# Expert rows loaded by SyncE from a register address and turned by VectorE

## The chip, the cores and the metric

The kernel runs on one core of one Trainium2 chip. The metric is device time in microseconds (us) of one execution. Engines are called by their short names: PE (TensorE, matrix products; PEld is its weight load), DVE (VectorE), ACT (ScalarE), POOL (GpSimd) and SP (SyncE, which here only issues transfers and relays semaphores). Sixteen DMA engines move data between HBM, the chip's DRAM, and SBUF, the on-chip memory of 128 partitions. Transfers issued by SP go through a hardware queue (q1 in the profile), those issued by POOL through a software queue (q0). PSUM holds matrix results.

## The reference

Eight images of 256 channels x 32 x 32 pixels go through two layers. Layer 0 is attention with 8 heads over the pixels. Layer 1 is attention with one head, and then a mixture of experts: each of the 8 x 1024 tokens is sent to its two best experts out of eight.

```python
# layer 1, mixture of experts, on tokens of 256 values
logits = tokens @ router_w.T
rw, re = top_k(softmax(logits), 2)
rw = rw / maximum(rw.sum(-1), 1e-12)          # two gates per token
out = tokens
for e in range(8):
    h = gelu(tokens @ w1[e] + b1[e])          # 256 -> 256
    out = out + gate[:, e:e+1] * (h @ w2[e] + b2[e])   # 256 -> 256
```

All data are float32.

## The kernel before

The images are worked off one after the other (`for b in range(B)`): `layer0` is the attention with 8 heads, `attend` the attention with one head, `normed` and `dispatch` the normalisation and the routing. For the first seven images `dispatch` writes each token's row of 256 values to DRAM twice, with an indirect DMA by POOL, into `rows`, where each expert has a region of its own. The rows of the last scatter leave during `layer0` of image 7. Image 7 itself is worked densely at the end (`dense`: all eight experts).

Between `layer0` and `attend` of image 7 stands the stage that the change is about, `experts` (L1018). The rows of the seven images are cut into 63 blocks of 256 rows (`BR`, which is `R` = 2 times 128); a block belongs to one expert. `plan` (L926) has worked out on DVE, for every block, where its rows begin (`row_at`) and which expert's weights it needs (`w_at`). For each block:

- `fetch` (L1024) lets POOL gather the block's weights, 128 rows of 5128 bytes out of `wpack`, into one of four buffers (`wb_0` to `wb_2` and `wb_x`, chosen by `b % 4`). Where block b needs the same expert as block b-4, the indices are out of bounds and nothing is moved. Then POOL gathers the block's 256 rows into `xr` (three buffers), so that partition p holds rows 2p and 2p+1. Four PE transposes write them to PSUM (`px`, L1044), and DVE copies them to `xb` (L1046, two buffers): channels on the partitions, tokens along the row.
- `hidden` (L1049): four products give `ph` (L1054), ACT applies Gelu (L1064).
- `collect` (L1073): four products give `pe` (L1079), DVE adds the bias (`yb`, L1088), SP stores the block to `y` (L1093).

A float32 product of 128x128 by 128x256 shows as two MATMUL records in the profile, so `ph` and `pe` have 8 records per block each, and `px` has 4. The loop works one block ahead: at step b it traces `hidden(b-1)`, `fetch(b)`, `collect(b-2)`. PE's order through the stage is therefore ph(b-1), px(b), pe(b-2), ph(b), px(b+1), pe(b-1), and so on.

What sets the order: the program is traced in order, and a scheduler then gives each engine its own list, in which an instruction may move ahead of earlier ones that are not ready in the scheduler's model of time. On the chip each engine works its list strictly in order. `tc.issue_after(ins)` places what is traced in its block behind `ins` on the same engine, without a wait for its end.

Three other places matter. In `layer0` of images 1 to 7 SP relays a semaphore after each half group of products (`relay.nop()`, L551), and the next group's first product waits for it. `pack` (L281) fills `wpack` early in the program, on SP's queue behind 56 MB of zeros for `rows` (`fill`, L266): two transfers for w1 (L286), two for w2 (L291), one for b1, eight for b2 (L302). Behind these stand, on the same queue, the transfers of `attend` of image 0 (`aT`, L697), where a quarter of the squares that DVE transposed are moved between partitions by SP. DVE transposes 32x32 squares within each partition group (`nc.vector.transpose`, L690, L430, L1219).

Of the kernel before, what the change touches and what calls it, by code (L numbers as in the profile page):

```python
# [10 lines left out]
F32 = mybir.dt.float32  # L11
# [8 lines left out]
def kernel(  # L20
# [23 lines left out]
    nc = tc.nc  # L44
# [14 lines left out]
    WROW = NCC * FF + NFC * D + NFC + D  # L59
    NWB = 3  # L60
    NXB = NWB + 1

    dram = ctx.enter_context(tc.tile_pool(name="dram", bufs=1, space=bass.MemoryType.DRAM))
    const = ctx.enter_context(tc.tile_pool(name="const", bufs=1))
# [10 lines left out]
    def big(name):  # L75

        return ps_big.tile([P, 1024], F32, tag="big", name=name)
# [58 lines left out]
    for e in range(E):  # L136
# [15 lines left out]
    r_iota = const.tile([P, 1], F32, name="r_iota")  # L152
    nc.gpsimd.iota(
        r_iota, [[1, 1]], base=0, channel_multiplier=R, allow_small_or_imprecise_dtypes=True
    )
    ones = const.tile([P, P], F32, name="ones")
    nc.gpsimd.memset(ones, 1.0)

# [48 lines left out]


    NB = NT // NH2
    SQ = 32  # L210
    NQ = P // SQ

    def bcast(t, n):

# [66 lines left out]
    def pack():  # L281


        wp = wpack.rearrange("(e p) c -> e p c", p=P)
        for dc in range(NCC):
            nc.sync.dma_start(  # L286
                wp[:, :, ts(dc, FF)], w1.rearrange("e (dc p) f -> dc e p f", p=P)[dc]
            )
        at = NCC * FF
        for fc in range(NFC):  # L290
            nc.sync.dma_start(  # L291
                wp[:, :, at + fc * D : at + (fc + 1) * D],
                w2.rearrange("e (fc p) d -> fc e p d", p=P)[fc],
            )
# [142 lines left out]
    def layer0(b, xT, begun, routing, xs):  # L437
# [138 lines left out]
        for at in range(last + LAG + 1):  # L576
            g, j = steps[min(at, last)]

            early = at > LAG and j == 1 and (g, j) not in PROJECT
            if at <= last:  # L580
                with tc.issue_after(counted.ins) if counted else nullcontext():
                    score(at, 0, 0)
            if 0 < at <= last + 1:
                with tc.issue_after(counted.ins) if counted else nullcontext():
                    score(at - 1, 1, 1)
                second_max(at - 1, 1)
                soften(at - 1, 1)
            if at >= LAG:
                with tc.issue_after(counted.ins) if counted else nullcontext():
                    gather_values(at - LAG, 0)  # L590
                counted = None
            if at <= last:

                with tc.issue_after(seconds[1].ins) if 1 in seconds else nullcontext():
                    first_max(at, 0)
                score(at, 0, 1)
                score(at, 1, 0)
                second_max(at, 0)
                if not early:
                    soften(at, 0)  # L600
                with tc.issue_after(seconds[0].ins):
                    ahead = divide(at - 1) if at > 0 else seconds[0]
                with tc.issue_after(ahead.ins):
                    first_max(at, 1)
            elif at == last + 1:
                divide(last)
            if at == 0:
                begun.rest()
                share()
            if at >= LAG:  # L610
                array = gather_values(at - LAG, 1)
# [314 lines left out]
    def plan(group):  # L926
# [51 lines left out]
        nc.vector.tensor_copy(row_at[:, :nb], lo)  # L978
# [36 lines left out]
                ats.append(at)  # L1015
            group.kept[b] = gate, ats

    def experts(group):  # L1018
        n = group.n
        row_at, w_at = group.where  # L1020

        wbs_x = [*wbs, one.tile([P, WROW], F32, tag="v", name="wb_x")]

        def fetch(b):  # L1024
# [10 lines left out]
            nc.gpsimd.indirect_dma_start(  # L1035
                out=xr.rearrange("p r d -> p (r d)"),
                out_offset=None,
                in_=group.rows[:, :],
                in_offset=bass.IndirectOffsetOnAxis(ap=row_at[:, b : b + 1], axis=0),
            )  # L1040
            px = big(f"px_{n}_{b}")
            for dc in range(NCC):
                for r in range(R):
                    nc.tensor.transpose(px[:, ts(dc * R + r, P)], xr[:, r, ts(dc, P)], ident)  # L1044
            xb = two.tile([P, NCC, BR], F32, tag="xb", name=f"xb_{n}_{b}")
            nc.vector.tensor_copy(xb.rearrange("p c t -> p (c t)"), px[:, : NCC * BR])  # L1046
            return xb

        def hidden(b, xb):  # L1049
# [23 lines left out]
        def collect(b, hT):  # L1073
# [19 lines left out]
            nc.sync.dma_start(group.y[ts(b, BR), :].rearrange("(p r) d -> p r d", r=R), yb)  # L1093
            if b == NXB:
                with tc.issue_after(added.ins):
                    places(group)


        rows, hiddens = {}, {}
        for b in range(group.nb + 2):  # L1100
            if b - 1 in rows:
                hiddens[b - 1] = hidden(b - 1, rows.pop(b - 1))
            if b < group.nb:
                rows[b] = fetch(b)
            if b - 2 in hiddens:
                collect(b - 2, hiddens.pop(b - 2))

    class Results:

# [235 lines left out]
    for b in range(B):  # L1345
# [6 lines left out]
        if b + 1 < B:  # L1352
# [64 lines left out]
```

## Time and profile before

| what | us |
|---|---|
| median of 15 runs (lowest, highest) | 2361.88 (2359.56, 2366.89) |
| the profiled execution's own time | 2363.75 |
| its span from first to last instruction | 2361.6 |
| experts: first `ph` product to the last `pe` record (1877.5 to 2131.1) | 253.6 |
| from the first `ps` product of image 0's `attend` to that of image 1 | 248.0 |
| from the first `ps` product of image 1's `attend` to that of image 2 | 240.1 |

The profile's page gives busy time per engine and the chain of work that ended last; the trace can be asked for instructions in order of time, for the DMA queues in a stretch, and for busy shares in stretches. A busy PE record can overlap the next one, so the time that a group costs is read from the distance between starts, and not from the durations.

### The profile page before, as it was taken

The page shows a single profiled execution, that of the slowest core. Times are in us where ns is not written, and L with a number is a line of the kernel's source. Part 1 is how long each engine was busy: PE and PEld are TensorE (multiplying, and loading weights), DVE is VectorE, ACT ScalarE, POOL GpSimd, SP SyncE. Part 2 cuts the span into 40 slices and gives each one's busy share as a digit, 9 for nine tenths or more (in the row PEclk, how much of TensorE's full clock was granted, in tenths as well). Part 3 has the DMA queues.
Part 4 walks back from the last instruction along what each step waited for, and adds up shares of the span by engine and source line. Part 5 has one row for each costly group of instructions (what it writes and reads, how often), then busy time and mean ns, then how long its engine had stood idle before and what let it go on. Part 6 is the DMA issues. An engine that isn't in the chain of part 4 may idle for free.

```text
span 2361.6 us, 37255 instructions
## 1 busy us (share of the span) xinstructions
PE 2305.2 (98%) x13375; PEld 1256.6 (53%) x13375; DVE 1512.4 (64%) x3660; ACT 1092.4 (46%) x1954; POOL 421.3 (18%) x391
## 2 busy tenths in 40 slices
PE   9999999999999999999999999999999999999798
PEld 3345534653455345634563356335633588885465
DVE  5775577567855785578557855786578653334755
ACT  3663366346634663466346634663555422223311
POOL 0000012000200020002000200030003144444563
PEclk9999999999999999999999999999999999999899
DMA  8995201020102010201020102010201266655564
GB/s 295 385 386 140 63 17 39 13 50 15 41 10 54 12 44 7 57 10 46 4 60 6 50 1 50 17 35 1 45 19 63 86 223 215 206 195 145 154 176 110
DMA packets 219232, 209.23 MB, mean 89 GB/s; under 512 B 120200, under 2 KB 162856, under 8 KB 217256
## 3 DMA queue, kind: packets, MB, share of 16 engines
q1 hardware_dynamic: 192952, 139.13, 19.6%
q0 software_dynamic: 25008, 67.20, 9.2%
q8 instruction: 107, 1.75, 0.3%
q10 hardware_dynamic: 1088, 0.52, 0.1%
q14 instruction: 77, 0.63, 0.1%
HBM read 108.88 MB, written 110.90 MB: 93 GB/s over the span
## 4 chain that ended last, share of the span: by engine, by line
PE 89%; DVE 5%; DMA 2%; issue 2%; another core or an unknown queue 1%; ACT 1%; SPq 0%; DVEq 0%; ACTq 0%; POOLq 0%
PE po L541 19%; PE psc L464 19%; PE py L713 8%; PE ps L672 8%; PE pqk L346 7%; PE pr L638 5%; PE pv L383 4%; PE ph L1054 4%; PE pe L1079 4%; PE px L657 2%; PE pqk L324 2%; PE pdy L1307 2%; PE pdh L1283 2%; PE px L1044 1%
## 5 line engine op out<-in xcount | busy, mean ns | idle before, releaser
L505 ACT ACTIVATE ex<-psc,nmax 128x1024 f32<-128x1024 f32 x512 | 570.5, 1115 | 304.4 <-DVE scrap L488 218.0
L464 PE MATMUL psc<-qk,qk 64*64 64x512 f32 x4096 | 575.7, 593 | 7.8 <-ACT ex L505 7.7
L541 PE MATMUL po<-ex,vs 64*64 64x512 f32 x4096 | 569.7, 592 | 1.4 <-DVE vs L521 0.5
L488 DVE TENSOR_SCALAR_CACHE_REDUCE scrap<-psc,nmax 128x512 f32<-128x512 f32 x512 | 384.2, 750 | 161.2 <-PE psc L464 134.9
L479 DVE TENSOR_REDUCE nmax<-psc 128x1 f32<-128x512 f32 x512 | 350.3, 684 | 9.5 <-PE psc L464 9.5
L464 PEld LDWEIGHTS psc<-qk,qk 64*64 64x64 f32 x4096 | 179.3, 132 | 285.1 <-ACT ex L505 136.4
L541 PEld LDWEIGHTS po<-ex,vs 64*64 64x64 f32 x4096 | 174.3, 132 | 275.5 <-issue 85.0
L713 PE MATMUL py<-n,aT 128*128 128x256 f32 x1024 | 235.7, 384 | 7.5 <-DVE aT L706 3.9
L672 PE MATMUL ps<-nT,xa 128*128 128x512 f32 x512 | 228.6, 592 | 0.0
L713 PEld LDWEIGHTS py<-n,aT 128*128 128x128 f32 x1024 | 197.0, 193 | 59.2 <-issue 27.0
L917 POOL DMA_INDIRECT rows<-n,d_at x112 | 109.2, 975 | 660.8 <-DVE nmax L479 660.5
L844 POOL TENSOR_TENSOR t<-t,n 128x2048 f32<-128x2048 f32 x8 | 36.3, 4535 | 879.7 <-DVE n L238 879.7
L697 ACT COPY aT<-sq 32x256 f32<-32x256 f32 x384 | 154.4, 402 | 82.0 <-DVE sq L690 44.1
L346 PE MATMUL pqk<-xT,wqkv 128*128 128x512 f32 x384 | 171.2, 599 | 0.0
L672 PEld LDWEIGHTS ps<-nT,xa 128*128 128x128 f32 x512 | 96.6, 190 | 102.4 <-issue 94.7
L680 DVE TENSOR_REDUCE nmax<-ps 128x1 f32<-128x1024 f32 x64 | 77.9, 1217 | 84.9 <-PE ps L672 82.7
L311 ACT ACTIVATE qk<-pqk,b_qks 128x512 f32<-128x512 f32 x124 | 85.6, 691 | 95.5 <-PE pqk L346 77.0
L1163 POOL DMA_INDIRECT yk<-y,yat x112 | 111.3, 994 | 90.5 <-issue 29.4
L346 PEld LDWEIGHTS pqk<-xT,wqkv 128*128 128x128 f32 x384 | 71.0, 190 | 99.9 <-issue 76.8
L383 PE MATMUL pv<-wqkv,xT 128*128 128x512 f32 x256 | 121.3, 602 | 1.0 <-DVE v L391 1.0
L638 PE MATMUL pr<-wo,res 128*128 128x256 f32 x512 | 111.9, 379 | 0.3 <-ACT res L560 0.3
L1064 ACT ACTIVATE hb<-ph,wb 128x256 f32<-128x256 f32 x96 | 40.3, 471 | 147.4 <-issue 80.3
(191 smaller groups left out, 2444.8 us busy)
## 6 DMA issues: line engine op xcount, KB each, us to landing
rows<-wb SPq DMA_DIRECT2D x7, 8192.0 KB
y<-yb SPq DMA_DIRECT2D x63, 256.0 KB
aT<-sq SPq DMA_DIRECT2D x384, 32.0 KB
xs<-in_x_dram SPq DMA_DIRECT2D x64, 128.0 KB
out_dram<-oT SPq DMA_DIRECT2D x60, 128.0 KB
xT<-in_x_dram SPq DMA_DIRECT2D x7, 1024.0 KB
sums<-t SPq DMA_DIRECT2D x7, 1024.0 KB
o<-sums SPq DMA_DIRECT2D x7, 1024.0 KB
```

Of the source, the lines that this page charges most:

```text
L346: mm = nc.tensor.matmul(pq[:, ts(n, 512)], wqkv[:, cc, t, ts(g, P)], xT[:, cc, ts(n, 512)], start=(cc == 0), stop=(cc == NCC - 1),)
L383: nc.tensor.matmul(pv, self.xT[:, cc, ts(i, P)], wqkv[:, cc, 2, :], start=(cc == 0), stop=(cc == NCC - 1),)
L464: mm = nc.tensor.matmul(pss[at, h][ts(c, DK), ts(n, 512)], k[r, j * P + c * DK : j * P + (c + 1) * DK], q[r, ts(n, 512)], start=True, stop ...
L479: firsts[at, h] = nc.vector.tensor_reduce(nmax, pss[at, h][:, ts(0, 512)], AX.X, ALU.max, negate=True)
L488: seconds[h] = nc.vector.tensor_scalar(scrap, pss[at, h][:, ts(1, 512)], -1.0, nmaxes[at, h], ALU.mult, ALU.min, accum_out=nmax,)
L505: nc.scalar.activation(ex, pss.pop((at, h)), AF.Exp, bias=nmaxes.pop((at, h)), scale=1.0, accum_out=sums[at][:, h : h + 1],)
L541: mm = nc.tensor.matmul(po[n][ts(h, DK), :], vss[at][keys, h, :], exps[at, h][keys, ts(n, 512)], start=(j == 0 and turn == 0), stop=(j == ...
L638: nc.tensor.matmul(pr[:, :C], res[:, g, ts(i, P)], wo[:, g, :], start=(g == 0), stop=(g == NPAIR - 1))
L672: nc.tensor.matmul(psc[:, ts(n, 512)], xa[:, ec, ts(i, P)], nT[:, ec, ts(n, 512)], start=(ec == 0), stop=(ec == NCC - 1),)
L697: move(to[ts(k, SQ), a], since[ts(a, SQ), k])
L713: nc.tensor.matmul(py[:, :D], aT[m], n1[:, m, :], start=(m == 0), stop=(m == NT - 1))
L1163: ins = nc.gpsimd.indirect_dma_start(out=self.slot(at)[:, k, :], out_offset=None, in_=self.group.y[:, :], in_offset=bass.IndirectOffsetOnAxis(
```

## The change

The gather of rows, the PE transposes and the copy out of PSUM go. SP reads the block's first row number into a register (`value_load`) and issues four transfers from that address; each brings a quarter of the channels (64 values, 256 bytes) of all 256 rows to 32 partitions, so that partition 32k+t holds rows t, 32+t, 64+t, ... of quarter k. One DVE transpose of 32x32 squares then gives `xb`. A channel d = 64k + 32c + j so stands on partition 32k + j in half c; `pack` writes w1's rows in that order, in eight transfers in place of two. The rows of a block are no longer paired on a partition, and the store to `y` is written as two runs of 1 KB per partition in place of one of 2 KB. `plan` drops the partition's part of the row number and clamps it 256 rows below the end. The loop has one step more: at step b it traces `hidden(b-2)`, `fetch(b)`, `turned(b-1)`, `collect(b-3)`. The DVE transposes stand behind the last `divide` of `layer0` on DVE's list.

```diff
     def pack():
         wp = wpack.rearrange("(e p) c -> e p c", p=P)
-        for dc in range(NCC):
-            nc.sync.dma_start(
-                wp[:, :, ts(dc, FF)], w1.rearrange("e (dc p) f -> dc e p f", p=P)[dc]
-            )
+        src = w1.rearrange("e (k cc c) f -> k cc e c f", k=NQ, c=SQ)
+        for k in range(NQ):
+            for cc in range(NCC):
+                nc.sync.dma_start(wp[:, ts(k, SQ), ts(cc, FF)], src[k, cc])
...
-                divide(last)
+                evicted["divided"] = divide(last)
...
-        nc.vector.tensor_scalar(base, first, -float(BR), r_iota, ALU.mult, ALU.add)
+        nc.vector.tensor_scalar_mul(base, first, -float(BR))
...
-        nc.vector.tensor_scalar_min(lo, lo, float(cap - R))
+        nc.vector.tensor_scalar_min(lo, lo, float(cap - BR))
...
-    def experts(group):
+    def experts(group, behind):
...
-            xr = rowp.tile([P, R, D], F32, tag="xr", name=f"xr_{n}_{b}")
-            nc.gpsimd.indirect_dma_start(
-                out=xr.rearrange("p r d -> p (r d)"),
-                out_offset=None,
-                in_=group.rows[:, :],
-                in_offset=bass.IndirectOffsetOnAxis(ap=row_at[:, b : b + 1], axis=0),
-            )
-            px = big(f"px_{n}_{b}")
-            for dc in range(NCC):
-                for r in range(R):
-                    nc.tensor.transpose(px[:, ts(dc * R + r, P)], xr[:, r, ts(dc, P)], ident)
+            xr = rowp.tile([P, RUN, DQ], F32, tag="xr", name=f"xr_{n}_{b}")
+            with tc.issue_after(loads[-1].ins) if loads else nullcontext():
+                at = nc.sync.value_load(
+                    row_at[0:1, b : b + 1], min_val=0, max_val=E * group.cap - BR
+                )
+            mine = group.rows[bass.ds(at, BR), :].rearrange("(s t) (k d) -> k t s d", s=RUN, k=NQ)
+            for k in range(NQ):
+                loads.append(nc.sync.dma_start(xr[ts(k, SQ)], mine[k]))
+            return xr
+
+        def turned(b, xr):
             xb = two.tile([P, NCC, BR], F32, tag="xb", name=f"xb_{n}_{b}")
-            nc.vector.tensor_copy(xb.rearrange("p c t -> p (c t)"), px[:, : NCC * BR])
+            with tc.issue_after(behind.ins):
+                nc.vector.transpose(
+                    xb.rearrange("p cc (s t) -> p s cc t", t=SQ),
+                    xr.rearrange("p s (cc c) -> p s cc c", c=SQ),
+                )
             return xb
...
-            nc.sync.dma_start(group.y[ts(b, BR), :].rearrange("(p r) d -> p r d", r=R), yb)
+            nc.sync.dma_start(group.y[ts(b, BR), :].rearrange("(r p) d -> p r d", r=R), yb)
...
-        for b in range(group.nb + 2):
-            if b - 1 in rows:
-                hiddens[b - 1] = hidden(b - 1, rows.pop(b - 1))
+        for b in range(group.nb + 3):
+            if b - 2 in rows:
+                hiddens[b - 2] = hidden(b - 2, rows.pop(b - 2))
             if b < group.nb:
                 rows[b] = fetch(b)
-            if b - 2 in hiddens:
-                collect(b - 2, hiddens.pop(b - 2))
+            if b - 1 in rows:
+                rows[b - 1] = turned(b - 1, rows.pop(b - 1))
+            if b - 3 in hiddens:
+                collect(b - 3, hiddens.pop(b - 3))
...
-        experts(groups[0])
+        experts(groups[0], evicted["divided"])
```

`SQ` is 32, `NQ` and `DQ` are 4 and 64, `RUN` is 8.

More of the change, by code (lines that the diff above doesn't have):

```diff
@@ L61 @@
     NXB = NWB + 1
+    SQ = 32
+    NQ = P // SQ
+    DQ = D // NQ
+    RUN = BR // SQ
     dram = ctx.enter_context(tc.tile_pool(name="dram", bufs=1, space=bass.MemoryType.DRAM))
@@ L151 @@
     )
-    r_iota = const.tile([P, 1], F32, name="r_iota")
-    nc.gpsimd.iota(
-        r_iota, [[1, 1]], base=0, channel_multiplier=R, allow_small_or_imprecise_dtypes=True
-    )
     ones = const.tile([P, P], F32, name="ones")
@@ L209 @@
     NB = NT // NH2
-    SQ = 32
-    NQ = P // SQ
     def bcast(t, n):
@@ L1016, in places @@
             group.kept[b] = gate, ats
-    def experts(group):
+    def experts(group, behind):
         n = group.n
         row_at, w_at = group.where
+        loads = []
         wbs_x = [*wbs, one.tile([P, WROW], F32, tag="v", name="wb_x")]
@@ L1033, in fetch @@
             )
-            xr = rowp.tile([P, R, D], F32, tag="xr", name=f"xr_{n}_{b}")
-            nc.gpsimd.indirect_dma_start(
-                out=xr.rearrange("p r d -> p (r d)"),
-                out_offset=None,
-                in_=group.rows[:, :],
-                in_offset=bass.IndirectOffsetOnAxis(ap=row_at[:, b : b + 1], axis=0),
-            )
-            px = big(f"px_{n}_{b}")
-            for dc in range(NCC):
-                for r in range(R):
-                    nc.tensor.transpose(px[:, ts(dc * R + r, P)], xr[:, r, ts(dc, P)], ident)
-            xb = two.tile([P, NCC, BR], F32, tag="xb", name=f"xb_{n}_{b}")
-            nc.vector.tensor_copy(xb.rearrange("p c t -> p (c t)"), px[:, : NCC * BR])
+            xr = rowp.tile([P, RUN, DQ], F32, tag="xr", name=f"xr_{n}_{b}")
[8 more added lines that the diff above has]
+        def turned(b, xr):
+            xb = two.tile([P, NCC, BR], F32, tag="xb", name=f"xb_{n}_{b}")
+            with tc.issue_after(behind.ins):
[3 more added lines that the diff above has]
+                )
             return xb
```

## The prediction

> **What bounds the kernel now.** I read the page first: which engine is busy, and what the chain that ended last is made of.
>
> ```profile
> PE 2305.2 (98%) x13375; PEld 1256.6 (53%) x13375; DVE 1512.4 (64%) x3660; ACT 1092.4 (46%) x1954; POOL 421.3 (18%) x391
> PE 89%; DVE 5%; DMA 2%; issue 2%; another core or an unknown queue 1%; ACT 1%; SPq 0%; DVEq 0%; ACTq 0%; POOLq 0%
> ```
>
> PE is busy 98% and is 89% of the chain, so PE work taken away is worth its time, as far as nothing else steps in. Next, the instructions in order of time in the middle of the expert stage.
>
> ```profile
> 1946.84 0.60 PE L1044 MATMUL px<-ident,xr 128*128 128x128 f32 x4
> 1947.28 1.89 PE L1079 MATMUL pe<-wb,hb 128*128 128x256 f32 x8
> 1947.48 0.69 DVE L1046 COPY xb<-px 128x512 f32<-128x512 f32 x1 [1.47 <-PE px L1044]
> 1949.01 1.89 PE L1054 MATMUL ph<-xb,wb 128*128 128x256 f32 x8
> 1950.74 0.60 PE L1044 MATMUL px<-ident,xr 128*128 128x128 f32 x4
> ```
>
> The starts lie 0.44 us (px), 1.73 (pe) and 1.73 (ph) apart: a block costs PE 3.90 us, and none of it is idle. Third, busy time in stretches (after the length: PE, PEld, DVE, ACT, POOL; then clock, DMA share, GB/s), and pieces of the chain of waits in this stage.
>
> ```profile
> 196.33:444.33 248.00, 242.79 (x1464) 121.28 (x1462) 162.98 (x405) 126.92 (x224) 24.72 (x18) 0.99 0.18 45
> 444.33:684.45 240.12, 239.44 (x1464) 119.99 (x1462) 163.90 (x406) 126.92 (x224) 24.62 (x18) 1.00 0.12 30
> 1877.50:2131.10 253.60, 247.70 (x1258) 214.59 (x1257) 99.75 (x207) 55.68 (x129) 116.12 (x118) 1.00 0.65 215
> 1905.80:1918.60 12.80, 12.11 (x61) 10.10 (x60) 11.11 (x55) 2.52 (x6) 5.97 (x7) 1.00 0.81 264
> ```
>
> ```profile
> 1966.23 6.72 DMA wb<-wpack,w_at
> 1973.08 1.97 PE ph L1054 x8
> ```
>
> In the expert stage PE idles 5.9 us of 253.6. At every change of expert four blocks bring new weights; such a stretch (1905.80) has the DMA engines 81% busy. There the chain goes through a weight load: 6.72 us from POOL's issue to PE's product. Image 0's round takes 7.9 us longer than image 1's with the same PE records; what differs is SP's queue, where the transfers of `attend` stand behind `pack`. The last view is SP's own queue and the DMA queue q1 in four stretches: 9.7 to 10.4 us (256-byte packets only, `b_v`), 493 to 499 (512 bytes, `xs`), 1870 to 2110 (the stage) and 184 to 203 (`wpack`).
>
> ```profile
> 492.32 4.00 SPq L423 DMA_DIRECT2D xs<-in_x_dram  x8
> 212.10 35.24 SPq L697 DMA_DIRECT2D aT<-sq  x48
> L1093 SPq DMA_DIRECT2D y<-yb x63: 319/320/344, 1885.5 to 2134.0; - x63
> L291 SPq DMA_DIRECT2D wpack<-in_L_ffn_w_dram x2: 6755/7009/7263, 183.6 to 190.4; - x2
> ```
>
> ```profile
> q1 hardware_dynamic: 528, 0.13, 83.5%
> q1 hardware_dynamic: 2364, 1.07, 103.0%
> q1 hardware_dynamic: 8352, 16.78, 18.3%
> q1 hardware_dynamic: 3092, 3.14, 54.6%
> ```
>
> Share x 16 engines x length / packets gives one packet: 17.7 ns for 256 bytes, 41.8 for 512, 84.1 for the 2 KB packets of the `y` stores.
>
> **The change part by part.** *PE.* The 63 x 4 transposes go. The first two blocks' stand at 1859.64 and 1862.81 in the tail of `layer0`, where PE waits anyway; 61 x 0.44 = **-26.8 us**. A block then costs PE 3.46 us. At the start ph(1) no longer waits for px(1) and its copy (ph(0) to ph(1) was 3.11 us), but pe(0) then waits for Gelu, whose table load ends at 1880.53; -0.6 us.
>
> *DVE.* The copy (0.69 us) becomes a transpose of half the size of the known ones (1.245 us for 128x1024), 0.62 us. With `yb` it is 1.3 of 3.46 us, hidden beside PE; were it exposed it would cost 0.6 a block. It runs one step ahead of `hidden`, with `xb` free since the `hidden` two blocks earlier. In the start it shares DVE with the normalisation, which ends at 1883.4; at worst ph(2) waits 0.9 us, which I leave in the range.
>
> *POOL* loses 63 gathers of 0.955 us, which stood behind the weight gathers; no gain, as those wait for `yb` and not for POOL.
>
> *The weight loads.* wb(b) is asked for after yb(b-4), and ph(b) needs it: between them PE has two steps, now 7.80 us, then 6.92. The load does not get shorter, so at each of seven changes of expert 0.88 us more lies open: **+6.2 us**. After one such wait the next three loads have the wait itself as cover, so I count one per expert.
>
> *DMA in the weight blocks.* Now 0.81 x 12.80 / 3 = 3.46 us of DMA time a block. A block's rows cost q0 about 0.85 us today (45.1% x 16 x 240 us for 33.34 MB in the stage); as 1024 packets they cost 1024 x 17.7 / 16 = 1.13 us, or with the 512-byte packet's 41.8 ns 2.7 us. So 3.74 us (up to 5.3) against PE's 3.46. I take the lower, the row of the same size. 0.28 us x 4 blocks x 7 experts is 7.8 us, but half of it falls into the wait just counted: **+3.5 us** (0 to 7.8; 52 with the 512-byte price). [...] `y` keeps its bytes in twice as many packets: up to 0.2 us a block, in the same bound.
>
> [...]
>
> *SP.* Per block four loads and a store. `xs`, the nearest (256 pieces from DRAM into 32 partitions), takes 0.50 us each; `aT` 0.73 with its waits. The store has 0.32, and with 256 pieces at most 0.5. The register load and its address arithmetic show nowhere: at least the 29 ns of a register move on POOL, at most the 1.65 us of the longest SP issue of this kind. From 4 x 0.50 + 0.35 + 0.03 = 2.4 to 4 x 0.73 + 0.5 + 1.65 = 5.1 us a block; I take 0.7 us for the register work and the `xs` pace, 3.2 us: under 3.46, so hidden, with 0.3 us of cover. Behind a waiting load on SP stand the `y` stores; nobody waits for these but the buffer of `yb` two blocks later and the results' gathers after the stage.
>
> *SP in the tail of `layer0`.* The loads of blocks 0 to 2 become ready when the last scatter lands (1839.87, when POOL's first gather went) and fall among the relays until 1861.7. Twelve x 0.50 = 6 us of SP; a relay held up 0.5 us is half covered, as PE's weight load stands 0.43 us ahead of its product (1848.48 and 1848.91). Between 0 and 6 us; I take **+1.5**.
>
> *`pack`.* Same bytes, six more transfers, in pieces of 32 rows. The four weight transfers' 4 MB go at 166 GB/s, so w1's half takes 12.6 us. Lower bound: no change. Upper: where this trace cuts a load into 32-row pieces it goes at 179 GB/s (`xs`) against some 410 for whole rows (`xT`), 2.3 times as long: +16 us. SP and the queue are serial, and `aT` of image 0 starts when `pack` is through (212.10, while its first square is ready at 207.2). Every us of delay there costs up to one. Nothing tells DRAM to DRAM in 32-row pieces; I take **+6**, nearer the lower end since each packet stays 1 KB.
>
> The row again: w1's 2 MB at 166 GB/s, 12.6 us. [...]
>
> Constants, the missing iota and `plan`'s changed operands: nothing, same number of DVE operations, under the same PE work of `layer0`.
>
> Sum: -26.8 - 0.6 + 6.2 + 3.5 + 1.5 + 6 = -10.2. The profiled execution took 2363.75 us (span 2361.6 and 2.15 around it); it would take 2353.6. It lies 1.9 above the median of 15 runs, so against those I say **2351.7**.
>
> **The rivals.** *`pack` takes most of it back.* For: image 0 already loses 7.9 us to this queue. Against: packets as long as before. With +12.6 in place of 6 the time is 2358.3. The page counts for it: chance 0.2.
>
> *SP becomes the bound, and the kernel slower.* At 0.65 us a load, 0.5 for the store and 1.1 for the register, SP needs 4.2 us a block: 62 x (4.2 - 3.90) = +18.6, the weight waits vanish under it (-4), `pack` and the tail +7.5: 2384. It decides above 3.9 us a block. For: five transfers and a register load in a queue that works in order. Against: `xs` at 0.50. Chance 0.15.
>
> *The rows come late anyway:* the scheduler puts a load behind the store of the block before, and then only two steps are left for issue, landing and turning. The period stays near 3.9, and with the tail and `pack` the time is 2363 to 2369. For: SP's order is the model's. Against: on POOL today the row gathers went ahead of waiting weight gathers (xr at 1880.08 and 1883.29 before wb at 1886.24). Chance 0.1.
>
> *Small packets choke the DMA engines:* 5.3 us in half of the blocks. That costs 4 x 5.3 + 4 x 3.46 = 35 us per expert instead of 32; 2390. Chance 0.05.
>
> **How the numbers follow.** The forecast has 0.5, with its own range 2342 to 2357 (`pack` from 0 to 9, contention 0 to 8). About 0.2% (4.7 us) is what can be told from no change. Faster: the forecast but for a rest, and a third of the `pack` rival, 0.54. Within: most of `pack`, a part of late rows, 0.24. Slower: SP, choked DMA and the rest of late rows, 0.22. Up to 2372 the range takes in `pack`, late rows and the mild end of SP; it leaves out 0.15 above and some 0.03 below.
>
> **What the profile after would show.** Right: ph and pe alone on PE, 3.46 us a block, one wait of 1.5 to 2 us for weights per expert; SP's loads at some 0.5 us; DMA share about 0.75. `pack` shows in the start of `aT` (212.10 before) and in image 0's round (248.0). Wrong if SP is never idle in the stage, if DVE's transposes wait for `xr`, or if PE in the last 20 us of `layer0` waits for SP's relays.

## The result, and the profile after

| | before | after |
|---|---|---|
| median, us | 2361.74 (47 runs) | 2382.14 (9 runs) |
| lowest to highest | 2355.95 to 2368.10 | 2379.59 to 2386.18 |
| span of the profiled execution | 2361.6 | 2378.3 |
| its own time | 2363.75 | 2381.11 |

The change makes the kernel slower: 1.0086 of the time before, 95% interval 1.0075 to 1.0097. The forecast was 2351.7 us, with a range of 2342 to 2372.

The page of the profile after, busy time and the chain that ended last, by engine:

```profile
PE 2290.5 (96%) x13123; PEld 1225.4 (52%) x13123; DVE 1508.4 (63%) x3660; ACT 1093.7 (46%) x1955; POOL 360.5 (15%) x327
PE 74%; SPq 8%; issue 8%; DVE 5%; ACT 1%; another core or an unknown queue 1%; DMA 1%; POOL 0%; DVEq 0%; ACTq 0%; POOLq 0%
```

The 252 PE records of the transposes are gone (13375 to 13123), and with them some PE time, but PE is now idle 88 us and not 56. Where, the windows tell. Columns as before: stretch and length; PE, PEld, DVE, ACT, POOL; clock, DMA share, GB/s. The first two are the rounds of images 0 and 1, the last two the stage from its first `ph` to its last `pe`, and its steady part.

```profile
196.30:442.92 246.62, 241.40 (x1464) 120.19 (x1463) 162.97 (x405) 126.92 (x224) 24.71 (x18) 1.00 0.18 45
442.92:683.04 240.12, 239.44 (x1464) 119.99 (x1463) 163.87 (x406) 126.91 (x224) 24.63 (x18) 1.00 0.12 30
1862.67:2154.23 291.56, 253.77 (x1093) 200.84 (x1093) 103.28 (x228) 59.32 (x133) 59.57 (x60) 0.99 0.66 185
1910.00:2140.00 230.00, 195.13 (x826) 153.69 (x827) 72.09 (x127) 43.66 (x104) 51.90 (x52) 0.99 0.69 191
```

Image 0's round is 1.4 us shorter than before (248.00), image 1's the same. In the steady part of the stage, where PE was idle for 2% of the time before, it is idle for 15%. The instructions in order of time show why (the rows of PEld and POOL are left out):

```profile
1989.74 1.89 PE L1057 MATMUL ph<-xb,wb 128*128 128x256 f32 x8
1989.94 0.69 DVE L1091 TENSOR_TENSOR yb<-pe,wb 128x512 f32<-128x512 f32 x1 [3.02 <-PE pe L1082]
1990.55 0.70 DVE L1046 STREAM_TRANSPOSE xb<-xr 128x512 f32<-128x512 f32 x1
1990.66 0.39 SPq L1096 DMA_DIRECT2D y<-yb  x1
1991.72 0.84 ACT L1067 ACTIVATE hb<-ph,wb 128x256 f32<-128x256 f32 x2 [3.50 <-issue]
1991.88 2.17 SPq L1040 DMA_DIRECT2D xr<-rows  x4
1992.24 1.99 PE L1082 MATMUL pe<-wb,hb 128*128 128x256 f32 x8 [0.61 <-ACT hb L1067]
1994.08 1.89 PE L1057 MATMUL ph<-xb,wb 128*128 128x256 f32 x8
```

Starts of `ph` lie 4.33 us apart, not 3.46. Behind `ph` of a block comes `pe` of the *same* block, and that must wait for the block's Gelu. From the start of `ph` to the start of `pe` it is now 2.50 us, where 1.73 are work: 0.77 us of waiting, in every block, with another 0.10 between `pe` and `ph`. The `xb` of the `ph` at 1994.08 is ready at 1991.25 (1990.55 and 0.70), and its weights are asked for at 1982.71; PE stands until 1992.24 all the same, and runs it behind that `pe`, in the order of its list. PE's instruction list says the same: up to block 5 it runs ph(b+1), pe(b) as before, but pe_6 stands ahead of ph_7, and from there on every block has its two groups side by side. Nothing in the diff orders PE's products; the scheduler did it.

The rest of what moved, from SP's queue and q1 (the first line is image 0's `attend`; the second the end of `layer0` of image 7; the third q1 in the stretch 1910 to 2110):

```profile
211.37 35.91 SPq L695 DMA_DIRECT2D aT<-sq  x48
...
1839.88 1.09 PE L539 MATMUL po<-ex,vs 64*64 64x512 f32 x8 [2.07 <-SPq L549]
...
q1 hardware_dynamic: 61848, 23.96, 45.5%
```

`aT` starts 0.7 us earlier than before, so `pack` in its new pieces costs nothing. PE waits 2.07 us for a relay that stands on SP behind the first row load, which waits for the last scatter. Of q1's 61848 packets in that stretch 46438 are row pieces of 256 bytes, and in the trace these take 17.8 ns each.

The span's 16.7 us split into stretches that every kernel here has. The second column runs from the first score product of image 7's `layer0` to its first output product `pr`, the third from there to the last `pe`. The part behind the last `pe` differs from chip to chip: on the one that ran four of the kernels it takes 205 to 210 us, elsewhere 224 to 234, and the kernel before is 2338.09 us there against 2360 to 2365. So times below go by the ratio to the kernel before on the same chip, and stages by their own length, each in the profiled execution. The ratios given, with 95% intervals, are not exactly the quotients of two medians.

| kernel | `layer0` to `pr` | `pr` to last `pe` | both | behind | ratio of times |
|---|---|---|---|---|---|
| before | 148.3 | 267.7 | 416.0 | 230.4 | 1 |
| after | 154.6 | 286.2 | 440.8 | 223.7 | 1.0086 |
| TensorE's order put right | 154.7 | 329.0 | 483.7 | 234.0 | 1.0296 |
| before, order of the change | 148.9 | 288.4 | 437.3 | 226.7 | 1.0083 |
| three lists put right | 156.1 | 263.7 | 419.8 | 224.1 | 1.0016 |
| rows gathered by POOL | 150.1 | 247.2 | 397.3 | 204.6 | 0.9924 |
| three lists, burst spread | 153.5 | 256.4 | 409.9 | 205.8 | 0.9986 |
| everything together | 148.9 | 256.2 | 405.1 | 205.0 | 0.9979 |
| the same, on another chip | 148.0 | 258.7 | 406.7 | 230.4 | 0.9953 |

So of the 16.7 us, -1.4 come from image 0's round, +24.8 from `layer0`'s tail and the stage, and -6.7 from what lies behind it. That last gain no part of the change explains; it stands again in a second profile of the changed kernel (224.0) and is gone in the last row (230.4). The granted clock over this part was 0.94 before, 0.95 and 0.94 in the two profiles of the changed kernel, and 0.93 in that last one; if the time went by the clock, which is an estimate, a hundredth of 230 us would be 2.3 us, so it can be a part of the difference at most. What sets either was not tried.

### The profile page after: what moved, and what is told of

Read it like the earlier page. It is cut to its first block, busy times and chain, and to the rows that moved or that the text cites. A ratio compares the mean times of both kernels' runs of the same rounds, so it can differ in the third digit from the quotient of the medians.

```text
span 2378.3 us, 37607 instructions
## 1 busy us (share of the span) xinstructions
PE 2290.5 (96%) x13123; PEld 1225.4 (52%) x13123; DVE 1508.4 (63%) x3660; ACT 1093.7 (46%) x1955; POOL 360.5 (15%) x327
## 4 chain that ended last, share of the span: by engine, by line
PE 74%; SPq 8%; issue 8%; DVE 5%; ACT 1%; another core or an unknown queue 1%; DMA 1%; POOL 0%; DVEq 0%; ACTq 0%; POOLq 0%
PE po L539 16%; PE psc L462 16%; PE py L711 8%; PE ps L670 7%; PE pqk L344 6%; SPq L268 5%; PE pr L636 4%; PE pv L381 4%; PE pe L1082 3%; PE ph L1057 2%; PE px L655 2%; PE pqk L322 2%; PE pdy L1312 2%; PE pdh L1288 2%; SPq L286 1%
## 5 line engine op out<-in xcount | busy, mean ns | idle before, releaser
L1082 PE MATMUL pe<-wb,hb 128*128 128x256 f32 x384 | 96.7, 396 | 25.2 <-ACT hb L1067 15.3
L1091 DVE TENSOR_TENSOR yb<-pe,wb 128x512 f32<-128x512 f32 x48 | 33.2, 691 | 133.1 <-PE pe L1082 133.1
```

Source lines behind the costliest of these rows:

```text
L1082: nc.tensor.matmul(py[:, ts(r, D)], hT[:, fc, ts(r, P)], wb[:, at + fc * D : at + (fc + 1) * D], start=(fc == 0), stop=(fc == NFC - 1),)
```

## The experiments

**The order alone, in both directions.** Two runs move nothing but PE's order. In the changed kernel `pe` of b is put behind `ph` of b+1:

```diff
+            with tc.issue_after(last[b + 1].ins) if b + 1 in last else nullcontext():
                 ... the eight matmuls of pe(b); last[b] is the last matmul of ph(b)
```

> The changed kernel, with the matmuls of a block's second layer (pe of block b) put behind the last matmul of the next block's first layer (ph of b+1) on TensorE, as the kernel before had them in its list; nothing else differs. Theory A (the loss is the order alone: in the list of the changed kernel ph and pe of one block stand back to back from block 6 on, so TensorE waits 0.77 us in every block for that block's Gelu): the steady period falls from 4.33 to 3.46 to 3.6 us a block, which over some 55 blocks is 40 to 48 us: 2334 to 2345 us. Theory B (SyncE's 3.4 us of issue a block, the addresses and four transfers and one store, or rows that land late, is a bound of its own close behind): the waits for Gelu go, and waits for the transposed rows take their place; the period stays at 3.9 to 4.3 us and the time at 2360 to 2382 us. Theory C (weights come late once a block is short: four weight buffers, 254 ns packets): waits of ph for the weight transfers, 3.6 to 3.9 us a block, 2345 to 2365 us.

In the kernel before, the converse: `ph` of b+1 is put behind `pe` of b.

```diff
+            with tc.issue_after(last[b - 1].ins) if b - 1 in last else nullcontext():
                 ... the matmuls of ph(b); last[b] is the last matmul of pe(b)
```

> The converse on the kernel before: its gather and TensorE transposes are kept, and the first matmul of a block (ph of b+1) is put behind the last matmul of pe of b, so that only the four transposes of another block (0.44 us) stand between ph and pe of one block. Theory A: TensorE then waits for Gelu in each block, 0.77 us less the 0.44 us of transposes: the period goes from 3.90 to 4.2 to 4.3 us, over 60 blocks 18 to 26 us slower than the kernel before, 2380 to 2388 us. Theories B and C, by which the order is no cause: within 5 us of the kernel before, 2357 to 2367 us.

The converse came out as theory A said: 2379.6 against 2360.12 us, 1.0083 (1.0066 to 1.0099), nearly the loss of the change itself. In order of time:

```profile
1990.30 1.89 PE L1055 MATMUL ph<-xb,wb 128*128 128x256 f32 x8
1992.03 0.60 PE L1044 MATMUL px<-ident,xr 128*128 128x128 f32 x4
1992.80 1.99 PE L1080 MATMUL pe<-wb,hb 128*128 128x256 f32 x8 [0.18 <-ACT hb L1065]
1994.63 1.89 PE L1055 MATMUL ph<-xb,wb_x 128*128 128x256 f32 x8
```

Again 4.33 us a block: `ph` to `pe` is 2.50 us whether 0.44 us of transposes stand between them or nothing. In this order the transposes stand in a wait that is there without them, and taking them off PE gains nothing.

But putting the order right in the changed kernel made it far worse: 2432.78 us, 1.0296 (1.0274 to 1.0317), 5.12 us a block. Theory A, as stated, fell.

```profile
2002.83 0.69 DVE L1092 TENSOR_TENSOR yb<-pe,wb_x 128x512 f32<-128x512 f32 x1 [3.81 <-PE pe L1083]
2003.44 0.70 DVE L1046 STREAM_TRANSPOSE xb<-xr 128x512 f32<-128x512 f32 x1
2004.20 1.99 PE L1057 MATMUL ph<-xb,wb 128*128 128x256 f32 x8 [1.40 <-DVE xb L1046]
...
2009.32 0.48 PE L1057 MATMUL ph<-xb,wb 128*128 128x256 f32 x1 [1.40 <-DVE xb L1046]
```

`yb` of block b runs, and only then the transpose that the very next `ph` needs. Before, DVE's list had xb(b+3) behind yb(b); the changed kernel's has xb(b+2) there. So the lists of PE and of DVE had both lost a block of lead, and PE's order fitted DVE's.

**Two suspects with the order forced.** With PE's order as in the first run, the tail's loads were put behind the last relay, and, apart from that, the 70 operations of `places` were given out five a block:

```diff
-            with tc.issue_after(loads[-1].ins) if loads else nullcontext():
+            with tc.issue_after((loads[-1] if loads else relay).ins):
```

> As the run with the order put right, and the first block's address and row loads on SyncE put behind the last of the relays that SyncE does for layer 0 of the last image (the nops of line 549), so that no relay stands behind SyncE's wait for the scattered rows. If the loads in that tail cost what the trace of the changed kernel suggests (TensorE idle 2.07 us at 1839.9 behind a relay, and the products of the tail 2.7 us later than before once the ten block matmuls that moved ahead of them are taken off), this is 2 to 3 us faster than the run with the order alone. If the block matmuls only fill other waits there, no difference within 1 us. If the first blocks then wait for their rows, because 14 us of products (pr) don't cover three loads of about 2.5 us, it is 1 to 4 us slower.

```diff
-            if b == NXB:
+            if b >= NXB:
                 with tc.issue_after(added.ins):
-                    places(group)
+                    next(steps, None)   # places(group) as a generator
```

> As the run with the order put right, and the computation of where each token's results lie (70 VectorE operations that stand in one burst behind the addition of block 4) given out five operations a block from block 4 on. If that burst holds up additions and transposes of blocks 5 to 9 on VectorE (periods of 5.75, 8.05, 6.7 and 5.07 us in the changed kernel, some 8 us over its steady 4.33), this is 6 to 12 us faster than the order alone. If the scheduler had these operations in VectorE's gaps anyway, no difference within 2 us. If five more operations a block bring VectorE's own turn (addition 0.69, transpose 0.70, five of about 0.1 us) into the path of these 14 blocks, it is up to 5 us slower than the order alone.

The tail shrank from 154.7 to 148.0 us, yet the time stayed: 2434.80 against 2432.78. What the first blocks had done in the tail they then did behind it. Spreading cost 10.8 us (2443.57): with DVE's turn already in PE's path, each operation added to it. Neither run says anything about the change by itself; both say that DVE was the path.

**Three lists put right.** Theory A2: the loss is lead that the scheduler gave away on PE, DVE and SP alike.

```diff
+            with tc.issue_after(turns[b + 3].ins) if b + 3 in turns else nullcontext():
                 added = nc.vector.tensor_add(yb, ...)
+            with tc.issue_after(loads[-1].ins):       # the loads of b+4
                 nc.sync.dma_start(group.y[ts(b, BR), :]..., yb)
-        for b in range(group.nb + 3):
+        for b in range(group.nb + 4):   # hidden(b-3), rows of b, turned(b-1), collect(b-4), weights of b
```

> The lists of three engines put right, not TensorE's alone. In the run with TensorE's order alone a block took 5.12 us, and TensorE waited for the transposed rows (xb, 1.4 us) because VectorE's list has the transpose that the next block needs (b+2) behind the addition of block b; and SyncE's list has the loads of block b+4 behind the store of block b, which waits for that addition. Here TensorE has ph of b+1 ahead of pe of b, VectorE the transpose of b+3 ahead of the addition of b, and SyncE the loads of b+4 ahead of the store of b (rows are fetched one block earlier, weights where they were). Theory A2 (the loss is the lead of the rows over the products, lost in the scheduler's lists, and not the work of any engine): 3.46 to 3.65 us a block, 2325 to 2348 us. Theory B (SyncE's own 3.4 us of issue a block, with a store whose wait stands in its way, is a bound): 3.7 to 4.3 us a block with waits for the rows' transfers ahead of the transposes, 2352 to 2380 us. Theory C (weights): ph waits for the weight transfers, 3.6 to 3.9 us a block at the change of an expert, 2345 to 2360 us.

> As the run with three lists put right, and the store of a block's result issued by ScalarE, not by SyncE, so that SyncE's list in the stage holds nothing but addresses and row loads. Theory A2: the same time as the run with three lists, within 4 us (ScalarE has two Gelus of 0.84 us together in a block). Theory B: SyncE loses 0.39 us of issue and its wait for the addition in each block, so this is 0.3 us a block or some 15 to 20 us faster than the run with three lists. A third way: the store's wait for the addition, on ScalarE, holds up the Gelu of the next block, and it is 5 to 20 us slower.

The first gave 2363.01 us, 1.0016 (0.9995 to 1.0036) of the kernel before: the change's loss is gone. The second, with the store issued by ACT, gave 2372.82, 1.0038 (1.0024 to 1.0051): no gain from taking the store off SP, so theory B falls. Why it is not equal stays open; in the profiled executions, the fastest of either run, its tail and stage are only 2.1 us longer. A quiet block, without new weights, of the run with three lists:

```profile
2020.23 1.89 PE L1085 MATMUL pe<-wb,hb 128*128 128x256 f32 x8
2021.96 1.89 PE L1059 MATMUL ph<-xb,wb_x 128*128 128x256 f32 x8
2022.07 0.71 DVE L1048 STREAM_TRANSPOSE xb<-xr 128x512 f32<-128x512 f32 x1 [2.67 <-DMA xr<-rows]
2023.64 0.39 SPq L1101 DMA_DIRECT2D y<-yb  x1
2023.68 1.89 PE L1085 MATMUL pe<-wb,hb 128*128 128x256 f32 x8
```

1.73 and 1.72 us between starts: 3.45 us a block, PE never idle, DVE waiting for rows at no cost. That is the block that the forecast counted on. Between quiet stretches come waits, 34 us over 3.45 in all: 12 around `places` (blocks 7 to 10, each from its `ph` to the next, take 5.37, 6.88, 8.19 and 5.22 us; the expectations count them one lower) and 22 further on, at the changes of an expert.

**Undoing one part, and moving one.** In the first of four runs the rows are gathered by POOL again, by row numbers a partition as before, and all else of the change is kept. Its rows then lie in an order that the squares don't fit, so it does the same work but does not compute the reference's results. In the second `places` is traced behind the stage. The last two build on the three lists.

```diff
-            with tc.issue_after(loads[-1].ins) if loads else nullcontext():
-                at = nc.sync.value_load(row_at[0:1, b : b + 1], ...)
-            ... four loads on nc.sync
+            nc.gpsimd.indirect_dma_start(out=xr..., in_=group.rows[:, :], in_offset=... row_at[:, b : b + 1] ...)
```

> The changed kernel with one part undone: a block's rows are gathered by GpSimd from an index a partition, as before (128 packets of 2 KB, and the offsets a partition put back), and nothing is loaded by SyncE; VectorE's 32x32 transposes, the turned weight pack, the later additions and the split store stay. The rows then lie the wrong way round for the squares, so what the expert products compute is not the reference's; the work is the same. Theory A2 (what cost the time is that the scheduler, with SyncE's loads in its model, gives the rows' lead away and puts ph and pe of one block back to back; the transposes and the pack cost nothing): TensorE's list keeps ph of b+1 ahead of pe of b, a block takes 3.45 us, with waits at the changes of an expert, 2325 to 2350 us. If the transposes on VectorE are the cause, the period stays near 4.33 us and the time near 2375 to 2385 us.

```diff
-            if b == NXB:
-                with tc.issue_after(added.ins):
-                    places(group)
...
         experts(groups[0], evicted["divided"])
+        places(groups[0])
```

> The changed kernel with the 70 VectorE operations that compute where the tokens' results lie moved from behind block 4 to the end of the stage, one place in the program changed. If this burst costs the 8.3 us by which blocks 5 to 8 of the changed kernel exceed 4.33 us, the stage has 4.33 us from block 6 on and the time is 7 to 9 us less, 2373 to 2376 us, less what the gathers of the results then wait for them (0 to 6 us). If the burst were what turns the order round, the blocks behind it would now take 3.45 us and the time would be 2330 to 2345 us.

> The run with three lists put right, and the same 70 operations given out two or three a block from block 4 on. In the run with three lists blocks 5 to 9 took 3.47, 5.37, 6.88, 8.19 and 5.22 us against 3.45: 11.9 us that the burst costs there. If VectorE has room for them (0.71 and 0.65 us of its own in 3.45), 9 to 12 us faster than the three lists, 2351 to 2355 us. If they push transposes into the path, no faster. The waits at the changes of an expert stay in either case: 16 DMA engines have 2.0 us of weights, 1.15 of rows in 256-byte packets and 0.8 of results in a block there, 4.0 us in all against 3.45.

> As the run with three lists and the 70 operations spread, and the first block's loads on SyncE behind the last of layer 0's relays. With TensorE's order alone this made no difference (2434.8 against 2432.8 us), where the block matmuls had room to fill in. If SyncE's loads hold the relays up by 2 to 3 us on the path, this is 2 to 3 us faster than the run without; if the matmuls of the first two blocks, which filled these waits, now stand behind the tail instead, within 1.5 us of it.

Rows by POOL: 2320.47 against 2338.09 us, 0.9924 (0.9908 to 0.9941). With SP's loads out of the program, the scheduler keeps ph(b+1) ahead of pe(b) without being told, and a quiet block takes 3.45 us with DVE's transposes in it:

```profile
1975.50 1.89 PE L1060 MATMUL ph<-xb,wb_x 128*128 128x256 f32 x8
1977.23 1.89 PE L1085 MATMUL pe<-wb,hb 128*128 128x256 f32 x8
1977.43 0.71 DVE L1049 STREAM_TRANSPOSE xb<-xr 128x512 f32<-128x512 f32 x1 [1.03 <-PE ph L1060]
1978.96 1.89 PE L1060 MATMUL ph<-xb,wb 128*128 128x256 f32 x8
```

So neither these nor `pack` cost anything that shows, and SP's loads are what the scheduler answered with its new order. The run takes out the register load, the four transfers and their `issue_after` at once; which of these turns the order was not tried.

Moving `places` missed its aim: nothing held it behind the stage, and the scheduler put it *ahead*, into `layer0`'s tail. The group of the first of its five operations, in this run and in the changed kernel (count: shortest, median, longest in ns, first and last start in us):

```profile
L999 DVE TENSOR_TENSOR p_hot<-exp,e_iota x14: 216/218/221, 1764.2 to 1822.1; 128x64 f32<-128x64 f32 x14
```

```profile
L999 DVE TENSOR_TENSOR p_hot<-exp,e_iota x14: 211/217/240, 1900.0 to 1913.6; 128x64 f32<-128x64 f32 x14
```

There it delays the last scatter by 8.2 us and the tail by 8.0 (162.6 against 154.6). In the stage, the excess of blocks 6 to 9 over 4.33 (5 to 8 in the expectation's count) falls from 8.2 to 2.4 us, and pe_6 still stands ahead of ph_7. Tail and stage together are 2.2 us longer than the changed kernel's (443.0 against 440.8); the ratio, 1.0132 (1.0116 to 1.0149) against 1.0086, is higher by more than that, on another chip, and why stays open. So the burst costs the stage some 6 us and isn't what turns the order.

Spread two or three a block, with three lists put right, the 70 operations take the excess of blocks 7 to 10 over 3.45 from 11.9 to 3.3 us: 2335.18 us, 0.9986 (0.9977 to 0.9996). The tail's loads behind the relays as well: 2332.02 us, 0.9979 (0.9970 to 0.9989), 4.8 us less up to the last `pe`. Both are faster than the kernel before. The spread is worth 0.0030 of the time, 7 us (9 to 12 were expected, and the runs with and without it are from two chips), the tail 3.2 us (2 to 3).

**What is left: the changes of an expert.** Two runs were to tell whether the DMA engines' time (D) or late issue (L) sets the waits there, each based on everything together.

```diff
+            with tc.issue_after(done.ins):      # done: the second Gelu
+                nc.scalar.dma_start(spare[ts(b, P), :], wqkv[:, 0, 0, : BR * D // P])
```

> The run with everything together (three lists, operations spread, first loads behind the relays) and one transfer more a block: ScalarE stores 256 KB of a constant tile to a spare buffer behind each block's Gelus; nothing waits for it. By the packets of the kernel before (128 of 2 KB at 85 ns over 16 engines) it is 0.68 us of every DMA engine's time in a block. Theory D (at the changes of an expert the 16 DMA engines are the bound: 2.0 us of weights, 1.15 of rows and 0.8 of results, 4.0 us a block for four blocks, against TensorE's 3.45): the some 28 blocks at changes grow by about 0.7 us each, 15 to 22 us in all against the run with everything together, and the others stay at 3.45 (they have 2.0 us of DMA time, then 2.7). Theory L (what is late there is the order: a weight load can't be issued before the addition of four blocks earlier, and a row load not before SyncE reaches it, with DMA engines to spare): 0 to 5 us slower.

```diff
-            mine = group.rows[bass.ds(at, BR), :].rearrange("(s t) (k d) -> k t s d", s=RUN, k=NQ)
+            mine = group.rows[bass.ds(at, BR), :].rearrange("(q t r) (k d) -> k t r q d", t=SQ, r=R, k=NQ)
...
-            nc.sync.dma_start(group.y[ts(b, BR), :].rearrange("(r p) d -> p r d", r=R), yb)
+            nc.sync.dma_start(group.y[ts(b, BR), :].rearrange("(p r) d -> p r d", r=R), yb)
```

> The run with everything together, with less DMA time in one place: the rows of a block are loaded in another order of tokens (still 256-byte runs, as many), so that a partition's two results are neighbours in memory and the store goes out as 128 packets of 2 KB, as in the kernel before, and not as 256 of 1 KB: 0.68 against 0.81 us of 16 engines a block. Theory D: 0.13 us in each of some 28 blocks at changes, 2 to 4 us faster than the run with everything together, near 0.9965 of the kernel before. Theory L: no difference within 1.5 us.

They ran on another chip than their base, 1.0210 and 1.0151 of the kernel before, so all were run again on one chip, with the changed kernel beside them.

> Everything together again, as the base of the next two, on one chip with them and with the changed kernel. Where weight packets take 253 ns, 0.997 to 0.999 of the kernel before, as it was; where they take 280 ns, theory D has the changes of an expert at 4.2 us a block and more, 5 to 10 us above, 1.000 to 1.004.

> Everything together and one transfer of 256 KB more a block, 0.68 us of every DMA engine's time, that nothing waits for. Theory D: some 28 blocks at changes grow by about 0.7 us each, 15 to 22 us above everything together on the same chip. Theory L: 0 to 5 us above it.

> Everything together with the store in 128 packets of 2 KB, not 256 of 1 KB, by another order of tokens in the row loads: 0.13 us of 16 engines less a block. Theory D: 2 to 4 us below everything together on the same chip. Theory L: within 1.5 us of it. A third way, that the loads' new order (rows two apart, in four pieces of two neighbours) is what made the run on the other chip 1.0151 of the kernel before: 10 us or more above everything together.

> The changed kernel, unaltered, on the same chip as the three others: 1.008 to 1.010 of the kernel before, as it was; its blocks of 4.33 us leave the DMA engines room at the changes of an expert (4.0 us), so a chip with slower weight packets moves it little.

Everything together: 2352.60 us against 2365.29 before, 0.9953 (0.9934 to 0.9972), and 2382.39 for the changed kernel (1.0075, 1.0056 to 1.0095). The two variants missed both theories: 2408.28 and 2398.05 us. The second came out as the third way of its expectation; the wide store costs 45 us. SP's queue says how; the wide store first, then everything together:

```profile
1967.00 0.54 SPq L1109 DMA_DIRECT2D y<-yb  x1
1968.35 2.94 SPq L1047 DMA_DIRECT2D xr<-rows  x4
1971.39 0.54 SPq L1109 DMA_DIRECT2D y<-yb  x1
```

```profile
1950.93 0.40 SPq L1103 DMA_DIRECT2D y<-yb  x1
1952.11 1.86 SPq L1044 DMA_DIRECT2D xr<-rows  x4
1954.08 0.39 SPq L1103 DMA_DIRECT2D y<-yb  x1
```

From store to store SP needs 4.39 us with the wide store and 3.15 without: the four row loads of a block take it 2.94 us to issue, not 1.86, a store 0.54, not 0.39. With 4.39 us back to back SP is the bound, and blocks take 4.6 us on average. That is the mechanism of the forecast's second rival; the changed kernel itself never gets there. Why the loads of that order take longer to issue wasn't tried.

The extra transfer did not load the DMA engines alone either. SP's own waits, in that run from 1900 to 2110 us (us in total, times, longest):

```profile
SPq L1105 <- DMA spare<-wqkv: 44.4, 20, 5.1
SPq L1044 <- DMA spare<-wqkv: 13.1, 8, 2.5
```

SP waits 57.5 us of the 210 for a transfer that ACT issued and whose data SP doesn't use; what ties SP to it was not tried. So neither run separates D from L. What does speak is the windows: everything together at a change and between two, and the gather by POOL at a change.

```profile
1928.50:1944.30 15.80, 13.53 (x62) 11.09 (x61) 6.39 (x18) 3.36 (x8) 3.10 (x4) 1.00 1.03 277
1946.00:1957.00 11.00, 11.00 (x53) 9.68 (x52) 6.41 (x16) 2.52 (x6) 3.00 (x3) 1.00 0.57 148
```

```profile
1926.80:1941.10 14.30, 12.72 (x60) 10.92 (x59) 4.96 (x8) 2.53 (x7) 6.84 (x8) 1.00 0.94 302
```

At a change the DMA share is 1.03, the engines busy without a break, and PE loses 2.3 us of 15.8; between changes the share is 0.57 and PE is never idle. With POOL's gather the share at a change is 0.94, and PE loses 1.6 us of 14.3. Full DMA engines are what theory D requires; a run that frees them and nothing else is missing.

## Why the prediction was wrong

The step that failed is its first term: "A block then costs PE 3.46 us." It took PE's work for PE's time, and so took for granted that ph(b+1) would stay between ph(b) and pe(b) in PE's list. That product is what covers Gelu. Without it, a block costs 4.33 us with or without transposes, as the converse run shows. What the runs put in its place: the scheduler answered SP's loads with less lead for the rows, in three lists.

- *PE, -26.8.* The size was right where the order holds: 3.45 us a block in the runs with three lists and with POOL's gather. In the changed kernel it was +0.44 us a block from block 10 on. A small misreading beside it: a block has four `px` records, and the two each at 1859.64 and 1862.81 are those of the first block alone, so the term would be 62 x 0.44, 27.3.
- *The start, -0.6.* It can't be read: `ph` of block 0 and part of block 1 now run in `layer0`'s tail.
- *DVE, 0.62 us a transpose.* It takes 0.70, and is hidden, as said.
- *Weight loads +6.2 and contention +3.5.* In the changed kernel both are zero, because 4.33 us a block cover them. With the order right they were undersized: all blocks' excess over the quiet block is 7.9 us before, 16.6 with POOL's gather and 23.7 with everything together on the same chip as that. By these differences less cover costs about 8.7 us (the kernel before may have been profiled on another chip), and the row loads as SP issues them, in small packets, about 7 more; no run changes one of the two alone. One wait per expert was too few: in the window shown the DMA engines are full through all four of its weight blocks.
- *SP, 3.2 us a block.* It measured 3.15 where SP goes from store to store without a wait. The second rival's condition was never met in the changed kernel; the wide store met it by accident.
- *SP in the tail, +1.5.* Undersized: the relay waits are there (2.07 us in one place), and with the loads behind the relays the run up to the last `pe` is 4.8 us shorter.
- *`pack`, +6.* It is zero or less: `aT` starts 0.7 us earlier, image 0's round is 1.4 us shorter. The first rival falls. No run shows its +12.6, the time of w1's half once more; in its place they show the queue through with `pack` 0.7 us earlier.
- *Packets of 256 bytes.* 17.7 ns were forecast and 17.8 measured, so the fourth rival falls. The 512-byte packets of `xs` take 46.1 ns (the forecast's 41.8 was an average with smaller ones). In the stage small packets are dearer by the byte all the same: four of 256 bytes take 71 ns, one 1 KB packet of the stores in the same stretch 50.6.
- *The third rival* was the nearest. It named the scheduler and the lead of the rows, but let the wait appear as late rows near 3.9 us a block. It appeared as a wait for Gelu, at 4.33.
- *Not foreseen:* the burst of `places`, which costs the changed kernel's stage some 6 us (12 over 3.45 us a block in the run with three lists), and the 6.7 us gained behind the stage.

Why the scheduler gave the lead away was not settled. SP's loads are the cause, as the run with POOL's gather shows, and the burst is not, as the run with `places` moved shows. That its model makes SP slower than it is on the chip is likely, since the rows land in time once the lists are forced, but this was only argued.

## What to carry to other kernels

Before counting work off the bound engine as time, write down which instruction of its list covers which latency, and ask whether the new list will still have it there. A new user of a queue can change the order on engines that it doesn't touch. When an order was lost, look for the same lost lead on every engine of the loop: put right on one of them alone, it cost another 50 us here; on all three it turned a loss of 0.9% into no loss, and with the burst spread and the tail's loads moved into a gain of 0.2 to 0.5%.

## What the runs showed of the hardware that was not expected

- The same number of row pieces, of the same size, in another order of tokens took SP 2.94 us a block to issue in place of 1.86; from store to store it needed 4.39 us in place of 3.15.
- A transfer that nothing needed held up another engine's transfers for 57.5 us (44.4 + 13.1) of a stretch of 210; what tied the two together was not tried.
- A register load from SBUF and its arithmetic took SP 0.28 + 0.15 us, not the 0.7 that the forecast had put; four loads and a store with it took 3.15 us.
- The part behind the stage took 205.0 us on one chip and 230.4 on another, with the same program (everything together); up to the last `pe` the two differ by 1.6 us (405.1 and 406.7).
